# Shifted-window attention and a Fourier layer on one core: the first two images get an order of their own

## The chip, the cores and the metric

The kernel runs on one NeuronCore of a Trainium2 chip. The metric is the device time of one execution, in microseconds (us). All times of the profile are counted from the start of the program's span. TensorE, VectorE, ScalarE and GpSimd are called PE, DVE, ACT and POOL in the profile, and SP is the engine whose queue issues most DMAs.

## The reference

The input has 32 images of 56 x 56 positions with 128 channels in float32. Two layers follow each other, and both are residual: `x = x + f(group_norm(x))`.

```python
# layer 0: windows of 7 x 7 after a roll by 3, 4 heads of 32 channels
xs  = roll(gn(x), (-3, -3));  win = xs cut into 64 windows of 49 tokens
q, k, v = win @ w_qkv.T;      q *= 32 ** -0.5
a   = softmax(q @ k.T + bias(rpb_table) + shift_mask)
x   = x + roll(merge(a @ v) @ w_proj.T + b_proj, (3, 3))
# layer 1: along the width and along the height
y   = dct(gn(x))[..., :32];  y = einsum("bixy,ioy->boxy", y, w);  z = idct(y)
b   = relu((z_width + z_height) @ W1 + b1) @ W2 + b2
x   = x + b
```

The group norms take mean and variance over groups of four channels of a whole image, so an image's attention can start only when all of it has been read, and its second layer only when all of its attention is done.

## The kernel before, in words

The unit of work is a window row: 7 lines of an image, 8 windows, 392 tokens. An image has 8 rows, so there are 256 rows in all. The program is written as cycles. Cycle r does the scores of row r, the division and transposition of earlier rows, the values and the projection of row r - 3, and the sums for the second norm of row r - 4. From cycle 11 (`CONV_BEGIN`) on the second layer of an image runs beside the attention of later rows: its step c is cycle 11 + c for image 0 and 8 cycles later for each next image. Steps 0 to 2 transform (`transform`, `turn_modes`, `scale_modes`), steps 3 to 5 mix the modes (`mix`, result `z`), steps 5 to 7, 10 and 12 transform back (`modes_back`, `fetch_back`, result `xf`), and seven steps from 8 on are the feed-forward (`ff_in`, `ff_out`).

The order of PE, ACT, DVE and POOL is the order in which the program issues, cycle by cycle, written out by hand (`manual_schedule`). For SP that holds for the first 11 cycles only; later the planner places SP's DMAs. Each engine works through its own list in order and waits where an input or a buffer isn't ready.

What the change touches:

- The start. Image 0 is loaded in quarters, with 32 columns of channels at a time (`load_quarter`, L156, 16 loads on two queues). DVE turns these into channels by tokens (`turn_quarter`, L351 to L356) and takes statistics of each row (`row_stats`, L373). `image_norm` makes from them `ve` (L417), `rstd` on POOL (L421) and the scaled weights `wn` on ACT (L429), which the first product needs. POOL's queue also loads the position bias: seven loads into `rpb_cols` (L205), seven copies from there (L209) and one of the result into the other half (L212). DVE adds mask and bias in pieces (`bias_and_mask`, L230).
- A row. `attn_q` and `attn_k` (L450, L463 on ACT), `attn_scores` (products L498, addition of bias on DVE L506), `attn_max` (DVE L516, subtraction on POOL L517), `attn_exp` (ACT L523), `attn_recip` (DVE L528 and L530), `attn_divide` on POOL (L536 into the same buffer, or L547 into `blocks`), `attn_transpose`, `attn_values` (products L592), `attn_project` (products L637, addition of the residual on DVE L645, store to `scr`), `attn_sums` (DVE L662), `attn_squares` (POOL L677 or ACT L679), `sum_squares` (DVE L683), `attn_v` (products L476).
- `attn_transpose` has two ways. For rows below `TURNED_BY_PE` (16) PE multiplies by an identity (L563) and ACT copies the result out (L570). For later rows DVE transposes blocks (L575), and POOL's division writes them in six pieces.
- The PSUM banks of attention and of the second layer are two rings of four, taken in turn (`attn_bank`, `conv_bank`).
- SP loads the residual tokens of a row two cycles ahead (`load_tokens`), POOL adds the projection's bias to them (`add_bias`, L138), `back_weights` issues 12 small loads in each of two cycles and `ff_weights` six.

The order of a cycle on DVE in the first 11 cycles, which the change rewrites:

```python
attn_sums(last, j)                    # row - 4
attn_scores(im, i, cycle); attn_max(cycle)
attn_squares(last, j); sum_squares(last, j); add_sums(last, j)
divide(cycle)                         # softmax sums and division of row - 1
turn(cycle)                           # row - 2
attn_project(im3, i3)                 # residual of row - 3
```

## Time and profile before

| what | value |
|---|---|
| median of 3 runs | 3230.74 us (3228.96 to 3234.39) |
| the profiled execution's own time | 3231.41 us |
| its span | 3229.6 us |
| PE busy | 3145.1 us (97%) |
| DVE, POOL, ACT busy | 2517.3, 2297.7, 2184.8 us |
| PE busy in the first 240 us | 170.53 us |
| first product of attention | at 24.98 us |
| DMA queues | 448.47 MB, mean 139 GB/s |

The page gives the busy time of each engine over the whole span. A matmul of float32 appears as two records. An engine that is mostly busy over the span can still be idle in one stage, so busy times are read by stage here. The column PEclk is the clock that TensorE was granted, as a share of the full one.

### The profile page before, as it was taken

The page shows a single profiled execution, that of the slowest core. Times are in us where ns is not written, and L with a number is a line of the kernel's source. Part 1 is how long each engine was busy: PE and PEld are TensorE (multiplying, and loading weights), DVE is VectorE, ACT ScalarE, POOL GpSimd, SP SyncE. Part 2 cuts the span into 40 slices and gives each one's busy share as a digit, 9 for nine tenths or more (in the row PEclk, how much of TensorE's full clock was granted, in tenths as well). Part 3 has the DMA queues.
Part 4 walks back from the last instruction along what each step waited for, and adds up shares of the span by engine and source line. Part 5 has one row for each costly group of instructions (what it writes and reads, how often), then busy time and mean ns, then how long its engine had stood idle before and what let it go on. Part 6 is the DMA issues. An engine that isn't in the chain of part 4 may idle for free.

```text
span 3229.6 us, 152033 instructions
## 1 busy us (share of the span) xinstructions
PE 3145.1 (97%) x65664; PEld 2348.3 (73%) x65664; DVE 2517.3 (78%) x4764; ACT 2184.8 (68%) x4004; POOL 2297.7 (71%) x2570
## 2 busy tenths in 40 slices
PE   5789999999999999999999999999999999999999
PEld 4567777777777777777777777777777777777776
DVE  7678887888887888887888887888888888888751
ACT  4466777666777676776676777666776666777664
POOL 5467777777777777777777777777777777777741
PEclk9899999999999999999999999999999999999999
DMA  7446566656566655566656566556656656565443
GB/s 128 96 118 146 140 141 147 140 143 146 136 143 146 144 141 142 141 143 144 144 138 145 140 144 145 143 137 145 143 141 145 148 135 146 143 143 142 123 137 103
DMA packets 1171652, 448.47 MB, mean 139 GB/s; under 512 B 527690, under 2 KB 1141116, under 8 KB 1170980
## 3 DMA queue, kind: packets, MB, share of 16 engines
q1 hardware_dynamic: 1162788, 437.41, 56.9%
q8 instruction: 514, 8.42, 1.2%
q10 hardware_dynamic: 7584, 1.18, 0.3%
q14 instruction: 158, 1.29, 0.1%
q0 software_dynamic: 608, 0.17, 0.0%
HBM read 277.00 MB, written 161.48 MB: 136 GB/s over the span
## 4 chain that ended last, share of the span: by engine, by line
PE 95%; POOL 1%; DVE 1%; ACT 1%; issue 1%; DMA 1%; SPq 0%; DVEq 0%; ACTq 0%; POOLq 0%
PE pc L124 41%; PE pa L124 10%; PE pa L476 8%; PE pc L803 7%; PE pa L498 6%; PE pa L637 6%; PE pa L592 6%; PE pc L842 5%; PE pc L756 4%; PE pc L563 1%; PE pc L929 0%; ACT k L463 0%; PE pa L703 0%; POOL a L517 0%; DMA zT<-zscr 0%
## 5 line engine op out<-in xcount | busy, mean ns | idle before, releaser
L547 POOL TENSOR_TENSOR blocks<-a,rs 32x272 f32<-32x272 f32 (+3 forms) x1434 | 1219.6, 858 | 384.9 <-DVE rs L530 274.6
L124 PE MATMUL pc<-wff,hid 128*64 128x128 f32 x12288 | 713.1, 273 | 1.6 <-issue 0.6
L124 PE MATMUL pc<-xf,wff 128*64 128x512 f32 (+2 forms) x3584 | 714.5, 539 | 0.0
L124 PEld LDWEIGHTS pc<-wff,hid 128*64 128x64 f32 x12288 | 680.0, 137 | 8.4 <-issue 4.2
L517 POOL TENSOR_TENSOR a<-a,mx 128x784 f32<-128x784 f32 x250 | 376.6, 1507 | 294.8 <-DVE mx L516 269.3
L124 PEld LDWEIGHTS pc<-xf,wff 128*64 128x64 f32 x3584 | 263.7, 136 | 370.3 <-issue 295.7
L887 ACT ACTIVATE hid<-pc,b1sb 128x512 f32<-128x512 f32 (+2 forms) x896 | 500.6, 642 | 41.9 <-PE pc L124 41.6
L124 PE MATMUL pa<-xw,wn 128*64 128x392 f32 x2048 | 392.5, 498 | 29.1 <-ACT wn L429 28.5
L506 DVE TENSOR_TENSOR a<-pa,bm 128x392 f32<-128x392 f32 x500 | 259.0, 560 | 168.2 <-PE pa L498 155.5
L483 ACT COPY v<-pa 128x512 f32<-128x512 f32 x256 | 152.0, 594 | 283.7 <-PE pa L476 275.1
L463 ACT ACTIVATE k<-pa,bqkv,heads 128x392 f32<-128x392 f32 x512 | 318.9, 674 | 15.3 <-ACT q L450 1.1
L138 POOL TENSOR_TENSOR xr<-xr,bproj 128x384 f32<-128x384 f32 (+1 forms) x256 | 292.9, 1144 | 47.2 <-DMA xr<-in_x_dram 24.5
L892 POOL TENSOR_TENSOR res<-res,b2sb 128x512 f32<-128x512 f32 (+1 forms) x224 | 252.1, 1126 | 77.7 <-DMA res<-scr 57.1
L778 ACT ACTIVATE y<-modes,rstd 128x448 f32<-128x448 f32 x256 | 276.6, 1138 | 41.8 <-DVE modes L771 31.4
L450 ACT ACTIVATE q<-pa,bqkv 128x392 f32<-128x392 f32 x256 | 149.8, 585 | 229.0 <-PE pa L124 227.2
L523 ACT ACTIVATE a<-a 128x784 f32<-128x784 f32 x250 | 214.0, 856 | 130.3 <-POOL a L517 130.0
L575 DVE STREAM_TRANSPOSE eT<-blocks 128x1024 f32<-128x1024 f32 x240 | 295.1, 1230 | 0.0
L592 PEld LDWEIGHTS pa<-eT,v 49*32 49x32 f32 x16384 | 173.0, 106 | 157.9 <-issue 70.8
L528 DVE TENSOR_REDUCE sm<-a 128x16 f32<-128x784 f32 x250 | 239.8, 959 | 56.0 <-ACT a L523 55.9
L476 PE MATMUL pa<-wn,xw 128*64 128x128 f32 x4096 | 281.8, 279 | 1.6 <-issue 1.2
L516 DVE TENSOR_REDUCE mx<-a 128x16 f32<-128x784 f32 x250 | 242.2, 969 | 7.7
L476 PEld LDWEIGHTS pa<-wn,xw 128*64 128x64 f32 x4096 | 219.8, 137 | 36.6 <-issue 2.3
(126 smaller groups left out, 4978.6 us busy)
## 6 DMA issues: line engine op xcount, KB each, us to landing
zscr<-z SPq DMA_DIRECT2D x512, 112.0 KB
xin<-in_x_dram SPq DMA_DIRECT2D x480, 112.0 KB
htok<-scr SPq DMA_DIRECT2D x128, 392.0 KB
zT<-zscr SPq DMA_DIRECT2D x192, 256.0 KB
res<-scr SPq DMA_DIRECT2D x160, 256.0 KB
out_dram<-res SPq DMA_DIRECT2D x160, 256.0 KB
scr<-x SPq DMA_DIRECT2D x256, 112.0 KB
xr<-in_x_dram SPq DMA_DIRECT2D x256, 84.0 KB
```

The costliest lines, as they stand in the source:

```text
L124: nc.tensor.matmul(dst[ps], lhsT=lhsT[:, ps], rhs=rhs, start=start, stop=stop)
L138: nc.gpsimd.tensor_tensor(piece, piece, bproj.unsqueeze(1).to_broadcast([P, n, C]), ALU.add)
L463: nc.scalar.activation(k_sb[:, u], pk[:, :RT].rearrange("p (w j) -> p w j", j=WT), AF.Identity, bias=im.bias[:, 3 + u : 4 + u], scale=head ...
L476: nc.tensor.matmul(pv[HALVES[w % 2], w // 2 * C : (w // 2 + 1) * C], lhsT=im.half[i // NP][:, t0 : t0 + JP], rhs=im.w[:, 2 * C : 3 * C], s ...
L506: nc.vector.tensor_tensor(a[:, 2 * hp : 2 * hp + 2, :, 0:WT].rearrange("p u w j -> p w u j"), ps[hp][:, :RT].rearrange("p (w u j) -> p w u ...
L517: nc.gpsimd.tensor_tensor(a3, a3, mx.unsqueeze(2).to_broadcast([P, 2 * NWR, WT]), ALU.subtract)
L547: nc.gpsimd.tensor_tensor(dst[to, k, :, :n], a3[src, :, kb * KB : kb * KB + n], rs[src].unsqueeze(2).to_broadcast([src.stop - src.start, 2 ...
L575: nc.vector.transpose(eT.rearrange("p t (k j) -> p k t j", k=2), blocks[r % 2])
L592: nc.tensor.matmul(po4[u][h * HD : (h + 1) * HD, pr], lhsT=v[ks, pr, h * HD : (h + 1) * HD], rhs=eT[ks, h * NP + pr, :WT], start=True, sto ...
L778: nc.scalar.mul(y[:, r], t.rearrange("p (n k) -> p n k", k=NM), im.rstd)
L887: nc.scalar.activation(hf[:, :n], ph[:, :n], AF.Relu, bias=b1sb[:, f : f + 1])
L892: nc.gpsimd.tensor_tensor(im.res[:, :k], im.res[:, :k], b2sb.unsqueeze(1).to_broadcast([P, k, C]), ALU.add,)
```

## The change

- **Start.** Image 0 is loaded by lines of tokens (`load_lines`, ten loads on the queues of SP and ACT) into the buffers `y_of`, and PE turns it: `turn_lines` multiplies each line by `turned_in`, an identity whose columns are rolled by three. ACT copies the result into the row layout, and DVE takes the statistics from PSUM.
- **Queues.** The copies into `rpb` move from POOL's queue to SP's (`place_rpb`), ahead of the loads of image 1. The loads of the second layer's transform matrices and of `gavg` move behind those of the mixing weights, and `bproj` moves from ACT's queue to SP's.
- **Rows 0 to 10** (`first_rows`). The division takes row r - 2 in place of r - 1 and stands early in the cycle. The squares of row r - 4 stand ahead of the subtraction, and the residual addition stands ahead of the softmax sums of the next division. Quarters and statistics of the next image move, and the norm's steps are taken earlier.
- **Rows 11 to 18** (`next_rows`). These cycles get an order of their own in place of the general one. The sums and scalings of the second layer are placed in it one by one, and the planner still places SP's DMAs.
- **Row 19.** The last cycle before the general order puts the squares of its finished row late and takes image 1's second statistics behind the feed-forward.
- **Transposition.** `TURNED_BY_PE` becomes 19, so rows 16 to 18 are transposed by PE too. The identity lies in `blocks[0]`, which POOL clears in cycle 20.
- Image 2's quarters are turned in cycles 8 and 9 with its statistics in 10, in place of cycles 8 and 9.

```diff
-TURNED_BY_PE = 2 * NWR
+TURNED_BY_PE = 2 * NWR + 3
...
-    for k in range(2):
-        for u in range(2):
-            xins[0, k, u] = load_quarter(0, k, u)
+    for n0, n1 in ((0, 2 * NQ), (2 * NQ, 3 * NQ), (3 * NQ, NCH)):
+        load_lines(n0, n1)
...
+    def turn_lines(im, p):
+
+        k = p // 2
+        slots = im.half[k][:, : NWR * WS * ROWS[k]]
+        slots = slots.rearrange("p (j h s) -> p h j s", j=NWR, s=WS)
+        banks = [(conv_bank, attn_bank)[k]() for _ in range(2)]
+        for n in range(NQ):
+            for r, ps in enumerate(LINE):
+                nc.tensor.matmul(
+                    banks[r][:, n * S : (n + 1) * S],
+                    lhsT=lines_of(p)[ps, n],
+                    rhs=turned_in[ps],
+                    start=True,
+                    stop=True,
+                )
+        for r, t in enumerate(banks):
+            h = 2 * NQ * p + r + (SS if k == 0 else WS - S // 2)
+            nc.scalar.copy(
+                slots[:, h : h + 2 * NQ - 1 : 2],
+                t[:, :RT].rearrange("p (n j s) -> p n j s", n=NQ, s=WS),
+            )
+            nc.vector.bn_stats(im.st[:, 2 * p + r], t[:, :RT])
...
     def first_rows(cycle):
...
+        divide_row(cycle - 2)
         if last:
-            attn_sums(last, j)
-        if cycle >= NWR:
-            next_quarter(cycle)
+            attn_squares(last, j)
...
+        attn_scores(im, i, cycle)
+        attn_max(cycle)
...
         if last:
-            attn_squares(last, j)
+            attn_sums(last, j)
             sum_squares(last, j)
             add_sums(last, j)
-        divide(cycle)
...
         turn(cycle)
         if im3:
             attn_project(im3, i3)
...
+    def next_rows(cycle):
+        c = cycle - CONV_BEGIN
...
+        attn_exp(cycle - 1)
+        scale_head(first, c, False)
+        next_quarter(cycle)
+        attn_values(im3, i3, cycle - 3, i in VALUES_BY_ACT)
+        tokens_bias(cycle)
+        if c == 0:
+            for h in range(2):
+                transform(first, True, h)
...
+        attn_scores(im, i, cycle)
+        attn_max(cycle)
+        for h in range(2 if c == 0 else 0):
+            for r in range(2):
+                turn_modes(first, True, h, r)
+        for r in range(2):
+            columns_turn(cycle, r)
+        turn(cycle)
+        for width, g in back_groups(c):
+            modes_back(first, width, g)
+            fetch_back(first, width, g)
+        if c == 3:
+            half_columns(cycle)
+        if c:
+            attn_squares(last, j)
+            attn_sums(last, j)
+        divide(cycle)
...
+        attn_v(im, i, cycle)
...
+        half_columns(cycle, True)
+        scale_head(first, c, True)
+        load_back(cycle + 1)
+        next_begin(cycle)
+        attn_project(im3, i3)
...
+    for cycle in range(CONV_BEGIN, HEAD_END):
+        next_rows(cycle)
+    for cycle in range(HEAD_END, NB * NWR + CONV_BEGIN + FF_AT[-1] - NWR + 1):
+        halves_first(cycle)
```

## The prediction

> **What bounds the kernel now.** I read the page first.
>
> ```profile
> span 3229.6 us, 152033 instructions
> PE 3145.1 (97%) x65664; PEld 2348.3 (73%) x65664; DVE 2517.3 (78%) x4764; ACT 2184.8 (68%) x4004; POOL 2297.7 (71%) x2570
> PE   5789999999999999999999999999999999999999
> PEclk9899999999999999999999999999999999999999
> ```
>
> TensorE is idle for 3229.6 - 3145.1 = 84.5 us, and the first slices hold most of it. So I asked for busy time by stage. Columns: stretch, its length, then PE, PEld, DVE, ACT, POOL busy, granted clock, DMA share, GB/s.
>
> ```profile
> 36.00:72.00 36.00, 28.13 (x768) 21.88 (x768) 26.32 (x46) 23.82 (x47) 18.80 (x16) 1.00 0.42 129
> 93.00:113.00 20.00, 13.71 (x344) 11.93 (x346) 12.55 (x21) 6.70 (x16) 7.79 (x7) 0.67 0.46 83
> 113.00:134.00 21.00, 15.11 (x366) 10.58 (x362) 12.88 (x24) 9.84 (x22) 13.13 (x12) 0.83 0.44 96
> 202.00:240.00 38.00, 34.58 (x836) 23.93 (x838) 29.88 (x61) 25.07 (x45) 31.25 (x36) 1.00 0.49 114
> 240.00:330.00 90.00, 89.33 (x1882) 68.12 (x1880) 72.97 (x136) 61.01 (x114) 66.79 (x75) 1.00 0.61 145
> ```
>
> The reader is to see that TensorE is full from 240 us on, and that no engine is full before. TensorE is busy 170.53 of the first 240 us, so 69.5 us are idle there: 25 ahead of its first product, 44.5 after. The clocks of all stages between 25 and 202 us add up to 41.4 us at half rate. Only these 240 us can be won.
>
> Then the timeline of the start, and the waits between 30 and 240 us (in total, times, longest).
>
> ```profile
> 14.61 3.88 POOL L209 DMA_DIRECT2D rpb<-rpb_cols  x7 [2.21 <-DMA rpb_cols<-in_rpb_rev_dram]
> 20.82 0.58 POOL L212 DMA_DIRECT2D rpb<-rpb  x1 [1.92 <-DMA rpb<-rpb_cols]
> 21.05 0.15 DVE L417 SCALAR_TENSOR_TENSOR ve<-back 128x1 f32<-128x1 f32 x1
> 23.68 0.60 POOL L421 TENSOR_TENSOR rstd<-ve,mhalf 128x1 f32<-128x1 f32 x1
> 24.98 1.57 PE L124 MATMUL pa<-xw,wn 128*64 128x392 f32 x4 [24.98 <-ACT wn L429]
> ```
> ```profile
> DVE part L683 <- POOL sq L677: 20.8, 10, 2.7
> PE pa L592 <- DVE x L645: 16.6, 6, 4.7
> DVE xw L351 <- DMA xin<-in_x_dram: 4.6, 2, 3.9
> ```
> ```profile
> 113.05 1.50 POOL L517 TENSOR_TENSOR a<-a,mx 128x784 f32<-128x784 f32 x1 [2.98 <-DVE mx L516]
> 114.51 1.04 POOL L677 TENSOR_TENSOR sq<-x 128x512 f32<-128x512 f32 x1
> 115.58 0.69 DVE L683 TENSOR_REDUCE part<-sq 128x32 f32<-128x512 f32 x1 [2.70 <-POOL sq L677]
> 116.18 0.96 DVE L528 TENSOR_REDUCE sm<-a_extra 128x16 f32<-128x784 f32 x1
> 117.35 0.56 DVE L645 TENSOR_TENSOR x<-pa,xr 128x384 f32<-128x384 f32 x1
> ```
>
> The start: `rstd` was ready to compute at 21.2 but waited 2.5 us behind the bias copies in POOL's queue. The rows: VectorE waits for the squares, which stand behind POOL's subtraction; behind that wait stands the residual addition L645, and behind it the PSUM bank that the next row's values need. I count rows by their row maxima L516: rows 0, 2, 10, 11, 18, 21 begin theirs at 31.86, 43.14, 121.22, 136.41, 217.02, 253.34. Rows 3 to 10 take 9.8 us each, the loop add 1.04, max 0.97, wait 2.6, sums 0.6, softmax sums 1.2, residual 0.65, values 0.8, scores 0.9 = 8.8, and what transposes of the next image (2.15) fall in it.
>
> **The start, part by part.** Image 0 came as 12,544 pieces of 128 B in 16 loads; now 3,136 of 512 B in ten. A packet of the middle of the run (600 to 700 us: 58.7% of 16 x 100 us by 37,077 packets, 377 B on average) takes 25 ns, so 3,136 x 25 / 16 = 5 us. Before, the last quarter reached VectorE at 14.90. The last rows are small loads which wait for loads eight earlier; I put their landing at 9 us (8 to 12). TensorE then turns the last seven lines. There are 56 turns, two records each. The nearest row is L563 (64 records of 49 columns, half as wide: 2.07 us), so all 112 take 4.1 us, 8.3 at half clock, of which the last quarter (2.1) lies on the path. ScalarE's two copies (L570, 0.5) add 1.1, the last statistics 0.5, the chain to `ve` 2.5 (18.72 to 21.20), `rstd` 0.6, weights 0.7: first product at 16.5, not 24.98. POOL no longer holds `rstd`: the eight bias copies go to SP, ahead of image 1's loads. They wait there for `rpb_cols`; landed at 14.6 before, about 11 now that the queues empty earlier. Then 7 x 0.42 issue, 2.3 landing, the copy of the copies 2.1: 18.4. Of 24 bias sums (L230, 4.74 us) 20 follow: 22.4. Row 0's scores are added then, not at 30.79: 8.4 us earlier (bounds 4 and 10).
>
> **Rows 0 to 10.** Rows 1 to 3 stay bound by VectorE (bias sums 2.86, transposes): maximum of row 3 at 42.2, before 50.15. From row 4, squares go ahead of the subtraction, the quotient is of two rows back, and the residual goes ahead of softmax sums. Two loops remain. TensorE: q and k 1.4, values 0.9, wait for ScalarE's k 0.35, scores 0.9, transposes 2.0, projection 0.8, v 0.9 = 7.25. VectorE: 1.04 + 0.97 + 0.6 + 0.6 + 0.6 + 1.2 = 5.0, plus 2.15 in the rows with a quarter = 7.2. I take 7.4. ScalarE (0.6 + 1.25 + 0.86 + 1.43 + 1.0 + 0.6 = 5.7) and POOL (1.5 + 1.5 + 1.2 + 1.0 + 0.3 = 5.5) stay under it. SP's 24 weight loads (53.72 to 61.86, 73.11 to 80.75) and six more (4.3) block stores and tokens as before, now in shorter rows: from row 2's store 59.5 SP reaches image 2's first quarter at 76.2, it is usable 5.3 later (94.17 to 99.51 before), and row 8 waits: 14 us, not 7.4. `nb`, on which TensorE waited 5.47 us there, is ready. Row 10 at 101, before 121.2: 20 us earlier. Moving gavg and dct behind w0 costs nothing: row 11 is the first to use them.
>
> **Rows 11 to 18.** Row 11: TensorE's transposes need a bank that VectorE frees only after two modes transposes: 9.3 of work + 3.3. Rows 12 to 18, each by its fullest engine: 9.5, 10.5, 12 (ScalarE: scale, shift, wrap, four z), 9.5, 11.8 (ScalarE: xf, z), 10.3, 11.5 (VectorE: statistics, xf) = 75.1; before 80.6. Row 18 at 188.6: 28.4 earlier.
>
> **Rows 16 to 18 by TensorE.** 3 x 2.07 = 6.2 us more of TensorE; VectorE loses 3 x 1.23, POOL 3 x 1.7. Bounds 0 and 6.2; two of the three fall where TensorE is full: 4.1. Clearing `blocks` (0.93 of POOL) and the later sums of row 19 lie under TensorE's work; uncovered, 1 to 2 us.
>
> **After row 21** every engine's instructions stand in the same order as before, so nothing per image changes.
>
> **The clock.** A gap of 2.71 us ahead of 72.39 was followed by half rate (L498 1.56 instead of 0.89 us); one of 2.02 at 61.2 was not. The Trainium skill, "TensorE: Matmul & The Clock Gate", section "HAM oscillation — how this bites in real kernels", sets the limit at idle gaps of about 3.4 us. By it only row 8's wait would be slow: some 5 us at half rate, 2 lost. By the row, row 11 and the gaps of rows 0 to 3 count too: 12 us, 4 lost. I take the row.
>
> **The sum**, by TensorE to row 21: before, 253.3 - 69.5 = 183.8 busy; 41.4 at half rate, about 0.71 busy, cost 14.7: 169.1 at full rate. After: start 16.5 + 169.1 + 6.2 + idle (rows 0 to 3 8.7, rows 4 to 10 8, row 11 3.3, rows 12 to 18 10.5, later 1 = 31.5) + clock 4 = 227.3: 26 us less. The rows' sum gives 28.4 - 4.1 = 24.3. I take 26.5: the profiled execution's own 3231.4 becomes 3204.9. The median of the runs, 3230.7, is 0.7 lower: 3204.
>
> **The rivals.** (1) Orders tighter than I think: rows 11 to 18 near TensorE's own 73 us, row 8 covered. Idle 17, clock 2: 211, 42 us less, 3189. For it: no engine's sum reaches its row. Against: in-order banks. Chance 0.14. (2) SP and ScalarE take the place: loads late in rows 5 to 8, each row 11 to 18 two engines in series, 12 us as before. Only start and rows 3 to 7 stay: 8 + 6 - 4 = 10 less, 3221. For it: SP's 8 us blocks, POOL's in-order token additions. Chance 0.10. (3) Slower: ScalarE in rows 11 to 18 becomes one chain with TensorE. Mixing waits for the scaling in front of it, and q for z behind it. Price: ScalarE's 10 to 11 us plus TensorE's 6.9 less what overlaps. It decides when these eight rows average 12 + (16 + 6.5) / 8 = 14.8 us against 12 now; at 15.5, 12 us slower, 3243. Against: rows 12 to 15 took 10 to 13 with the same work. Chance 0.03. (4) The turn isn't earlier, since small loads land late, and rows don't shorten: 3229. Chance 0.03.
>
> **How the numbers follow.** The forecast has 0.70. Its bounds (start 4 to 10, rows 0 to 10 by 5 us, rows 11 to 18 by 6, transposes 0 to 6) give 3192 to 3216; I reach to 3189 and 3219, leaving out about 1 in 10 on each side. A measurement here tells 0.2% (6.5 us) from no change. Faster takes forecast, (1), (2): 0.93 with a little left out.
>
> **What would show it.** First product by 18 us; L677's wait gone; rows 4 to 7 at 7.4 us; half clock under 15 us; row 18 before 195; from row 21 the same pace, 97 us an image. Wrong: row 18's maximum after 205, rows 4 to 7 above 9, or a different pace later.

## The result, and the profile after

| what | before | after |
|---|---|---|
| median, the changed kernel's own runs | 3230.47 us | 3222.48 us (3219.83 to 3228.9, 13 runs) |
| ratio, with its 95% interval | | 0.9976 [0.9967, 0.9984] |
| the same once more, in later runs (e12) | 3232.31 us | 3226.3 us, 0.9982 [0.9973, 0.9990] |
| the profiled execution's own time, span | 3231.41, 3229.6 us | 3222.57, 3220.8 us |
| first product of attention | 24.98 us | 23.31 us |

The change brings 6 to 8 us where 26.5 were forecast; 3219 was the upper end of what the prediction gave. These are lines of the page of the kernel after:

```profile
span 3220.8 us, 152669 instructions
...
PE 3162.6 (98%) x65968; PEld 2369.0 (74%) x65968; DVE 2508.5 (78%) x4753; ACT 2189.3 (68%) x4018; POOL 2280.0 (71%) x2552
```

TensorE is idle for 3220.8 - 3162.6 = 58.2 us instead of 84.5. So 26 us of idle time did go, about what the forecast's sum had. But TensorE is busy 17.5 us longer, and that is the sum to explain. Busy time by stage, the kernel after (columns: stretch, its length, then PE, PEld, DVE, ACT, POOL busy, granted clock, DMA share, GB/s):

```profile
5.40:18.30 12.90, 12.80 (x112) 12.49 (x112) 3.48 (x8) 3.70 (x9) 7.62 (x20) 1.00 0.46 90
...
82.00:102.00 20.00, 15.97 (x404) 13.50 (x404) 11.19 (x20) 10.29 (x25) 9.99 (x11) 0.84 0.63 130
...
227.00:317.00 90.00, 89.47 (x1906) 68.69 (x1904) 71.62 (x132) 61.00 (x116) 66.11 (x76) 1.00 0.60 141
```

The three rows are the turn, rows 8 and 9, and the 90 us from row 20's maximum on. The first is new: TensorE is full from 5.40 to 18.30 us with the 112 records of the turn, and its weight loads (PEld) are full too. In the second TensorE is idle for 4 us of 20, and the clock of 0.84 puts some 6 us at half rate (before, rows 8 and 9 had 0.67). The last reads like its counterpart of before: TensorE is full. Next, the start, from the timeline of the kernel after:

```profile
5.40 6.62 PE L400 MATMUL pc<-turned_in,y 56*128 56x56 f32 x55 [5.40 <-DMA y<-in_x_dram]
...
11.82 6.38 PE L400 MATMUL pa<-turned_in,y 56*128 56x56 f32 x55
...
20.18 10.99 SPq L160 DMA_DIRECT2D y<-in_x_dram  x16
...
21.81 0.15 DVE L486 SCALAR_TENSOR_TENSOR ve<-back 128x1 f32<-128x1 f32 x1
...
22.04 0.57 POOL L490 TENSOR_TENSOR rstd<-ve,mhalf 128x1 f32<-128x1 f32 x1 [6.23 <-DVE ve L486]
...
23.31 1.58 PE L129 MATMUL pa<-xw,wn 128*64 128x392 f32 x4 [5.11 <-ACT wn L498]
```

GpSimd no longer holds `rstd`: it waits 6.23 us for `ve`. But `ve` comes at 21.81, later than the 21.05 of before, because the turn ends at 18.2. The first product takes 1.58 us for four records, which is half rate. Image 1's loads start at 20.18 behind the bias copies (seven from 12.05 on, and the copy of the copies into the other half at 19.35). The waits between 30 and 240 us (in total, times, longest):

```profile
PE pa L661 <- DVE x L714: 10.1, 7, 3.4
...
DVE part L752 <- POOL sq L746: 3.2, 3, 2.1
```

The wait of VectorE for the squares fell from 20.8 to 3.2 us, and TensorE's for the residual from 16.6 to 10.1. Both were forecast. Other waits in rows 7 to 9 took their place (TensorE's timeline: start and length; in brackets how long it waited, and for what):

```profile
79.50 3.66 PE L632 MATMUL pc<-blocks,a_extra 128*64 128x49 f32 x64 [2.18 <-POOL a_extra L605]
...
100.00 3.65 PE L632 MATMUL pc<-blocks,a 128*64 128x49 f32 x64 [1.09 <-POOL a L605]
```

In row 7 TensorE waits for the quotient, because seven small instructions of the norm stand ahead of the softmax sum on VectorE. The transposes that follow take 3.66 us instead of 2.07: half rate. In row 8 VectorE waits 2.99 us, until 91.87, for image 2's quarter.

### The profile page after: what moved, and what is told of

Same layout as the page of the kernel before. It is cut to its first block, busy times and chain, and to the rows that moved or that the text cites. A ratio compares the mean times of both kernels' runs of the same rounds, so it can differ in the third digit from the quotient of the medians.

```text
span 3220.8 us, 152669 instructions
## 1 busy us (share of the span) xinstructions
PE 3162.6 (98%) x65968; PEld 2369.0 (74%) x65968; DVE 2508.5 (78%) x4753; ACT 2189.3 (68%) x4018; POOL 2280.0 (71%) x2552
## 4 chain that ended last, share of the span: by engine, by line
PE 94%; DVE 2%; issue 1%; DMA 1%; POOL 1%; ACT 1%; SPq 0%; DVEq 0%; POOLq 0%; ACTq 0%
PE pc L129 41%; PE pa L129 10%; PE pa L545 8%; PE pc L872 7%; PE pa L567 6%; PE pa L706 6%; PE pa L661 5%; PE pc L911 5%; PE pc L825 3%; PE pc L632 1%; DMA xin<-in_x_dram 1%; PE pc L998 0%; ACT k L532 0%; PE pa L772 0%; PE pc L400 0%
## 5 line engine op out<-in xcount | busy, mean ns | idle before, releaser
L616 POOL TENSOR_TENSOR blocks<-a,rs 32x272 f32<-32x272 f32 (+3 forms) x1416 | 1202.3, 856 | 379.1 <-DVE rs L599 257.1
L961 POOL TENSOR_TENSOR res<-res,b2sb 128x512 f32<-128x512 f32 (+1 forms) x224 | 251.8, 1124 | 83.4 <-DMA res<-scr 77.8
L847 ACT ACTIVATE y<-modes,rstd 128x448 f32<-128x448 f32 x256 | 276.8, 1141 | 44.8 <-DVE modes L840 31.3
L597 DVE TENSOR_REDUCE sm<-a 128x16 f32<-128x784 f32 x249 | 238.5, 958 | 45.9 <-ACT a L592 45.3
```

What stands on the lines that cost most here:

```text
L616: nc.gpsimd.tensor_tensor(dst[to, k, :, :n], a3[src, :, kb * KB : kb * KB + n], rs[src].unsqueeze(2).to_broadcast([src.stop - src.start, 2 ...
L847: nc.scalar.mul(y[:, r], t.rearrange("p (n k) -> p n k", k=NM), im.rstd)
L961: nc.gpsimd.tensor_tensor(im.res[:, :k], im.res[:, :k], b2sb.unsqueeze(1).to_broadcast([P, k, C]), ALU.add,)
```

## The stages, kernel by kernel

The table cuts each profiled execution at the maxima of rows 0, 10 and 21 and of the last row (255), in us. It holds the experiments too, which follow.

| kernel | row 0 at | rows 0 to 10 | rows 10 to 21 | row 21 to the last | ratio |
|---|---|---|---|---|---|
| before | 31.9 | 89.4 | 132.1 | 2833.5 | 1 |
| after | 30.9 | 80.2 | 130.5 | 2835.4 | 0.9976 |
| after, again (e12) | 30.4 | 83.4 | 133.3 | 2838.5 | 0.9982 |
| turn in halves (e1) | 27.2 | 79.7 | 136.0 | 2831.0 | 0.9970 |
| old start (e2) | 33.8 | 79.0 | 131.9 | 2833.6 | 0.9988 |
| old rows 0 to 10 (e3) | 31.0 | 95.9 | 134.2 | 2835.2 | 1.0033 |
| the same, image 2 as before (e14) | 30.9 | 89.1 | 133.7 | 2831.4 | 1.0019 |
| old rows 11 to 19 (e4) | 31.0 | 77.8 | 138.1 | 2835.3 | 0.9987 |
| rows 16 to 18 by DVE (e5) | 30.7 | 80.7 | 134.0 | 2830.2 | 0.9981 |
| products ahead of the turn (e6) | 31.3 | 79.9 | 136.3 | 2830.9 | 0.9970 |
| halves, bias on POOL's queue (e7) | 26.8 | 78.0 | 135.4 | 2828.8 | 0.9964 |
| and norm behind the sums (e8) | 27.1 | 80.1 | 134.9 | 2826.9 | 0.9962 |
| that again (e16) | 26.9 | 78.6 | 133.9 | 2825.9 | 0.9965 |
| that, last lines first (e11) | 28.6 | 79.1 | 137.6 | 2833.4 | 0.9972 |
| that, products behind the turn (e15) | 27.5 | 79.9 | 135.4 | 2830.2 | 0.9972 |
| new rows 0 to 10 alone (e9) | 34.1 | 80.1 | 134.4 | 2838.8 | 0.9988 |
| new start alone (e10) | 31.1 | 89.4 | 135.1 | 2831.2 | 1.0006 |
| new rows 11 to 19 alone (e13) | 33.7 | 89.9 | 144.6 | 2831.0 | 1.0036 |

The two profiles of the changed kernel differ by 5.6 us at row 21 and by 8.7 us at the last row. So one profile tells a stage's length to a few us, and the time is read from the ratios. The profiled execution isn't always one of middling time: in e1, e2, e14 and e16 it is the fastest of the kernel's runs, in e6, e9, e12 and e13 the slowest (e13's took 3246.08 us, with a median of 3237.4). The ratios tell two kernels apart only so far: the intervals of e2 and e4 touch both of those that the changed kernel has.

## The experiments

**The turn in halves (e1).** The theory here is that the turn sets the start, and not the landing of the loads. Each line's product is cut into two of 64 channels, the form of the row that the prediction had scaled.

```diff
-                    banks[r][:, n * S : (n + 1) * S],
-                    lhsT=lines_of(p)[ps, n],
+                    banks[r][hs, n * S : (n + 1) * S],
+                    lhsT=lines_of(p)[ps, n, hs],
```

> The changed kernel with each line turned in two halves of 64 channels instead of one product with 128 columns of weights. Weight theory: the turn takes 13.0 us because a record's weight load of 128 columns takes 330 ns and 56 lines have 112 of them; halves load into separate columns beside each other, the turn falls to 6 to 8 us, and the first product stands at 17 to 19 us instead of 23.3. Row 0's scores are then held by the bias sums (their input lands near 22.5), so row 0's maximum moves from 30.9 to 28 to 29 and the total falls by 2 to 3 us. Clock theory: the turn is slow because TensorE works at half rate until 34 us; halves leave it at 13 us or make it longer, the total within 1 us.

3222.45 us, 0.9970 [0.9959, 0.9982], not to be told from the changed kernel. The turn fell from 12.8 to 7.7 us (5.36 to 13.10), with twice as many records. A stretch of it in the columns of the busy times above, then two lines of the timeline:

```profile
6.70:11.70 5.00, 5.00 (x194) 5.00 (x190) 2.89 (x7) 2.98 (x6) 2.36 (x4) 1.00 0.79 152
```
```profile
5.36 3.70 PE L401 MATMUL pc<-turned_in,y 56*64 56x56 f32 x109 [5.36 <-DMA y<-in_x_dram]
...
18.53 1.58 PE L129 MATMUL pa<-xw,wn 128*64 128x392 f32 x4 [5.43 <-ACT wn L499]
```

In the trace's single records, two of the changed kernel's (one of each of two lines) start within 7 ns of each other, and the next two 213 ns later. In e1 four (two lines, two halves) start within 20 ns, and the next four 107 ns later. So four narrow records run beside each other where two wide ones do, and the turn's own pace is twice as fast; the rest of its 7.7 us is mostly waiting for lines.

The first product comes 4.8 us earlier, row 0's maximum 3.7. So the turn did set the start. At row 21 the lead over the changed kernel is gone (242.9 against 241.6), which lies within what two profiles of one kernel differ by.

**The old start (e2).** Loading by quarters and queues as before, everything else new.

```diff
-    for n0, n1 in ((0, 2 * NQ), (2 * NQ, 3 * NQ), (3 * NQ, NCH)):
-        load_lines(n0, n1)
+    for k in range(2):
+        for u in range(2):
+            xins[0, k, u] = load_quarter(0, k, u)
```

> The changed kernel with the start of the kernel before: quarters of 128-byte pieces, turned by VectorE, bias copies on POOL's queue, transform matrices early. Theory of the lost start: by the rows' maxima the new start is only 0.9 us ahead, so without it the total stays within 1.5 us of the changed kernel's. The prediction's view, that the start is worth 8 us: the total rises to about 3230.

3228.11 us, 0.9988 [0.9982, 0.9995]. Row 0 comes 2.9 us later than in the changed kernel and row 21 3.2 later. Leaving the new start out costs 2 to 4 us here, not 8.4. But this isn't quite the start of before. In the changed kernel the order written by hand holds from the first line of the program on (L86), in the kernel before only from the turning of image 0 on, and e2, e9 and e13 keep the new place. In their lists GpSimd's loads of the masks and its clears stand behind the bias copies, so `rstd` comes at 24.8 to 25.2 us (23.68 before) and row 0 about 2 us later than in the kernel before. So up to 2 us of the times of these three runs can be this list's.

**The old rows 0 to 10 (e3), and image 2 placed as before (e14).** In e3 `first_rows` has the old order. Image 2's steps stay where the change puts them: one quarter in cycle 8, one in 9. In e14 they go back too:

```diff
-        if b == 1:
-            steps[0] = ((0, 0), None, ())
-            steps[1] = ((0, 1), None, ())
-            steps[2] = (None, None, (0, 1, 2, 3))
```

> The changed kernel with rows 0 to 10 in the order of the kernel before. Order theory: the early squares, quotients and residual are worth the 9 us by which row 10's maximum came ahead; without them rows 3 to 10 take 9.5 us each again, and the total rises to 3230 to 3232. Rival: the time comes back in rows 11 to 18, which wait less then; the total rises by 3 us or less.

> The changed kernel with the old order of rows 0 to 10 as in the earlier run that was 10 us slower than before, but with image 2's two quarters and its statistics in cycles 8 and 9 as before, not in 8, 9 and 10. Theory 1, placing them later is what made rows 8 and 9 take 15 us each there (VectorE waited 15.3 us for quarters, SP reached them late): row 9 at 112 instead of 117, time at or below before (0 to 4 us less). Theory 2, the order of rows 11 to 18 behind old rows 0 to 10 does it: row 9 earlier or not, time still 8 us or more above before.

e3 took 3242.03 us, 1.0033 [1.0021, 1.0045]: slower than before. e14 took 3233.61 us, 1.0019 [1.0012, 1.0025]. Rows 0 to 10 take 95.9 us in e3, 89.1 in e14, 89.4 before. The old order and the new placing clash, and the cause is in the queue of SP. First e3, then e14 (SP's and VectorE's timelines):

```profile
107.37 0.78 SPq L722 DMA_DIRECT2D scr<-x  x2
...
108.31 3.55 SPq L160 DMA_DIRECT2D xin<-in_x_dram  x4
...
114.19 1.09 DVE L424 STREAM_TRANSPOSE xw<-xin 128x512 f32<-128x512 f32 x1 [6.12 <-DMA xin<-in_x_dram]
```
```profile
99.92 2.09 SPq L160 DMA_DIRECT2D xin<-in_x_dram  x4
```

In e3 the second quarter's loads stand behind a row's store at 107.37, which waits for its residual, and VectorE then waits 6.12 us for them. In e14 they leave at 99.92, ahead of that store (106.61). So the placing explains 7 us of rows 0 to 10, and by the ratios some 4.5 us of the time. It does not explain why e14 is still slower than before.

**The old order of rows 11 to 19 (e4).** The general order from cycle 11 on, as before, with PE transposing rows 16 to 18.

```diff
-    for cycle in range(CONV_BEGIN, HEAD_END):
-        next_rows(cycle)
-    for cycle in range(HEAD_END, NB * NWR + CONV_BEGIN + FF_AT[-1] - NWR + 1):
+    for cycle in range(CONV_BEGIN, NB * NWR + CONV_BEGIN + FF_AT[-1] - NWR + 1):
```

> The changed kernel with rows 11 to 18 in the general order of the later rows, as before. Order theory: the own order is worth the 8 to 9 us that its rows' maxima gained between row 10 and row 18, so the total rises to about 3231. Rival: the maxima stand earlier within their cycle in the own order, and 3 to 5 of these us are given back between rows 18 and 21; its worth is 3 to 5 us, total 3226 to 3227.

3227.98 us, 0.9987 [0.9980, 0.9994]. Rows 10 to 18 take 97.4 us against 86.7. A good part of that is no time: in the own order a row's maximum stands earlier among TensorE's work, and rows 18 to 21 then take 40.7 us against 43.7. From row 10 to row 21 it is 138.1 against 130.5 (133.3 in the second profile of the changed kernel, e12), and by the ratios 2 to 4 us.

**Rows 16 to 18 transposed by VectorE (e5).**

```diff
-TURNED_BY_PE = 2 * NWR + 3
+TURNED_BY_PE = 2 * NWR
```

> The changed kernel with rows 16 to 18 transposed by VectorE again (TURNED_BY_PE back at 16). Price theory: three rows cost TensorE 2.07 us each, and the lead of the rows' maxima falls by 7.4 us between rows 18 and 21, where TensorE is full; without them the total falls by 4 to 6 us, to about 3219 where the changed kernel has 3224. Rival: rows 16 to 18 aren't bound by TensorE, and VectorE's 1.23 us and POOL's division in pieces (3.2 instead of 1.5 us) make these rows longer by what TensorE saves; the total stays within 2 us.

3221.07 us, 0.9981 [0.9974, 0.9987]: not to be told from the changed kernel. TensorE's 6.2 us of transposes are gone, and yet nothing is won. GpSimd now divides these rows in six pieces of together 5.34 us, and rows 18 to 21 show what that holds (GpSimd and TensorE of e5, then the wait of VectorE between them: total, times, longest):

```profile
211.73 5.34 POOL L616 TENSOR_TENSOR blocks<-a,rs 128x512 f32<-128x512 f32 x6
...
220.65 1.08 PE L129 MATMUL pc<-xf,wff 128*64 128x512 f32 x4 [2.13 <-DVE res L1008]
```
```profile
DVE res L1008 <- POOL res L961: 6.3, 1, 6.3
```

The division stands ahead of the subtraction (217.15) and of `res` (218.61), VectorE waits 6.3 us for that, and TensorE waits for VectorE. Behind these waits TensorE stood at half rate (granted clock 0.53 from 222 to 233 us). Row 20's maximum comes 20.8 us after row 19's, against 15.2 in the changed kernel, where the division at this place is one instruction of 1.51 us (at 207.54).

So in the own order TensorE's transposes pay for themselves: they cost 6.2 us of TensorE and take about as much of waiting and half rate away.

**Products ahead of the turn (e6).** Three products of zeros with 512 columns, before the turn, so that TensorE is busy from 3.65 us on.

```diff
+    warm_up(3)
     images[0] = image_begin(0)
```

> The changed kernel with three more products of 512 columns on zeros ahead of the turn of image 0, which keep TensorE busy from about 4 to 8 us (their results are overwritten). Clock theory: TensorE is then at full rate when the lines arrive, and the second half of the turn takes 3.5 us instead of 6.4. Weight theory: the weight loads of 128 columns set the pace at either clock, the second half stays at 6 to 6.5 us. The total isn't expected to move by more than 3 us either way.

3218.01 us, 0.9970 [0.9958, 0.9981]. The turn in two halves of 56 records:

```profile
3.65 5.48 PE L169 MATMUL pa<-warm 128*128 128x512 f32 x6 [3.65 <-DVE warm L165]
...
9.07 3.33 PE L408 MATMUL pc<-turned_in,y 56*128 56x56 f32 x56
...
12.24 6.02 PE L408 MATMUL pa<-turned_in,y 56*128 56x56 f32 x56
```
```profile
12.30:18.20 5.90, 5.90 (x58) 5.78 (x56) 2.60 (x7) 1.95 (x4) 3.35 (x13) 0.51 0.08 15
```

The first half runs at 59 ns a record, the second at 108, as in the changed kernel (116), though TensorE was never idle between them. The clock granted to the second half was 0.51 of the full one. So the turn's price is the half rate and the wide form together. And the turn's own products, in this wide form, did not hold the full rate. The 5.5 us of products ahead of it took the gain away: the first product comes at 23.73.

**Halves, and the bias copies on POOL's queue (e7).** The seven copies into `rpb` go back to POOL's queue, behind the masks' loads, which move behind GpSimd's clears, so that image 1's first loads leave SP at once.

```diff
-                nc.sync.dma_start(
+                nc.gpsimd.dma_start(
                     rpb[iy * WS : (iy + 1) * WS], cols[:, :, WS - 1 - iy : span - iy]
                 )
-            nc.sync.dma_start(rpb[JP : JP + WT], rpb[0:WT])
...
+        if k:
+            nc.sync.dma_start(rpb[JP : JP + WT], rpb[0:WT])
```

> The turn in halves of 64 channels, and the position bias taken off SP: POOL issues the seven copies behind its memsets, SP only the last one, behind the first half of image 1's loads. Queue theory: in the turn in halves alone, image 1's loads start at 20.5 us because SP waits for the bias from 12 to 20 us, so tokens, mixing weights and with them rows 1 to 8 stay where they were; now they start near 11, end near 23, row 3's maximum moves from 47.8 to 44 or 45, and the total falls by 2 to 4 us against the halves alone. Rival: rows 1 to 3 are bound by VectorE's own work, and the early loads change nothing; total within 1.5 us of the halves alone.

3217.03 us, 0.9964 [0.9951, 0.9976]. Image 1's first loads start at 9.71 instead of 20.18, row 3's maximum comes at 45.3 (49.6 in the changed kernel) and row 10's at 104.8 (111.1). The last 14 records of the turn waited until 11.89 us for the last small loads. From 9.57 us on four records take 59 ns instead of 107: this turn reached the full rate. With e1 and e6 that gives the time from one group of records on two lines to the next (two records in the wide form, four in halves; the turn has 56 such groups):

| products with | at half rate | at full rate |
|---|---|---|
| 128 channels | 213 ns (changed kernel) | 112 ns (first half of e6) |
| halves of 64 | 107 ns (e1) | 59 ns (e7, 9.57 to 10.39 us) |

Width and clock each make a factor of about 2. And now the bias copies hold row 0 (VectorE's timeline of e7):

```profile
21.49 3.96 DVE L268 TENSOR_TENSOR bm<-rpb,mask 49x98 f32<-49x98 f32 x20 [1.63 <-DMA rpb<-rpb]
```

**And the norm step behind the sums (e8, again e16).** The seven small instructions that stood ahead of row 7's softmax sum move behind it.

```diff
         divide_row(cycle - 2)
+        if cycle == NWR - 1:
+            norm_step(cycle)
...
         attn_v(im, i, cycle)
-        if cycle == NWR - 2:
-            norm_step(NWR - 1)
```

> As the run before, and in cycle 7 the second step of image 1's norm (seven small instructions of VectorE) stands behind the softmax sums of row 5 instead of ahead of them. Theory: these seven delay POOL's quotient, TensorE waits 2.18 us at 79.5 for it and then goes to half rate for 6.8 us; moved, the wait falls under 1 us, no half rate follows in row 7, and the total falls by 2 to 4 us. Rival: row 8 waits for image 2's first quarter anyway, so what row 7 wins is waited there; the total stays.

> The fastest version once more, on the chip of the run with products between. If 0.9962 holds, 12 us below before, row 21's maximum at 240 to 243; if the earlier ratio was luck of scatter, 0.9970 to 0.9978 as the other kernels with the new rows.

3215.18 us, 0.9962 [0.9948, 0.9975], and in later runs 3215.82 us, 0.9965 [0.9951, 0.9978]. It is not to be told from e7. TensorE's wait in row 7 did fall, from 2.18 to 0.74 us, but row 8 then waited longer: from row 6's maximum to row 8's it takes 22.5 us in e7, 21.7 in e8, 22.7 in e16. The rival was right. The two runs agree, and with e7 they are the fastest found: about 11.5 us below before, where the changed kernel has 6 to 8. The intervals of the two kernels still touch.

**The new rows 0 to 10 alone (e9) and the new start alone (e10).** Each is the kernel before with one part of the change, and with the order by hand from the first line on: e9 has the edits of e2, e4 and e5 together, e10 those of e4, e5 and e14. The identity lies in a buffer of its own again, as before.

```diff
-    ident = blocks[0].rearrange("p k t c -> p (k t c)")[:, :P]
+    ident = work.tile([P, HB], F32, tag="hid", name="ident", bufs=NF)[:, :P]
```

> The kernel before with the new order of rows 0 to 10 alone: start, rows 11 to 18, row 19 and the transposes of rows 16 to 18 are the old ones. The knock-outs so far cost 4 (start), 18 (rows 0 to 10), 3.6 (rows 11 to 18) and 0 to 2 us (transposes), 26 in all against a gain of 8. Theory 1, the parts need each other and the knock-outs of the other three add: row 21's maximum at 241.6 + 3.2 + 5.3 + 3.9 = 254, time as before within 2 us. Theory 2, the order of rows 0 to 10 brings its gain by itself: row 10 at 112.8 as with the old start, then 96 us to row 18 as before, so row 18 at 209 and row 21 at 245, time 6 to 8 us below before. Theory 3, it brings by itself what leaving it out cost: 18 us below before.

> The kernel before with the new start alone (image 0 turned by TensorE, the bias copies on SP's queue); all rows in the old order. Theory 1, the start's gain is small and adds: row 0's maximum at 31 (before 31.9), row 10 within 2 us of 121, time 0 to 4 us below before. Theory 2, what made the kernel without the new rows 0 to 10 slower by 9 us is the new start, which lets image 1's loads come 1.6 us later than before and so holds rows 2 to 10: row 10 at 124 or later, time 5 us or more above before.

e9: 3228.18 us, 0.9988 [0.9979, 0.9996], 4 us below before, though its row 0 comes 2.2 us later (see e2). e10: 3234.31 us, 1.0006 [0.9998, 1.0015], no gain. In the stages the parts do add: the new rows 0 to 10 take 80.1 us alone and 80.2 within the change (before 89.4), and the new start alone gives a row 0 at 31.1 and leaves rows 0 to 10 at 89.4. So neither is held back by the other.

**The new rows 11 to 19 alone (e13).** The edits of e2, e5 and e14 together, so `next_rows` and row 19 as in the changed kernel, and all else as before but for the order by hand from the first line on. The loop that e4 took out is what stays:

```diff
+    for cycle in range(CONV_BEGIN, HEAD_END):
+        next_rows(cycle)
```

> The kernel before with the new order of rows 11 to 18 and of row 19 alone: start, rows 0 to 10 and the transposes of rows 16 to 18 are the old ones. Theory 1, this order by itself brings what leaving it out cost: row 11 to row 18 in 79 us instead of 80.6, row 10 unchanged at 121, time 4 us below before. Theory 2, this order does harm behind the old rows 0 to 10 (the kernel without the new rows 0 to 10 was 10 us slower than before, the new start alone about equal): time 5 to 10 us above before, row 18 at 222 or later.

3237.4 us, 1.0036 [1.0023, 1.0049]: 10 to 12 us slower than before; its row 0 already comes 1.8 us later (see e2). Rows 10 to 21 take 144.6 us instead of 132.1 in the profile, which is that of the slowest run. Two things stand in it. With VectorE transposing, row 20 again comes 20.8 us after row 19 (233.4 to 254.2), as in e5. And rows 11 and 12 run at half rate: the granted clock is 0.76 from 123 to 152 us, against 0.97 from 119 to 144 in e14. Both have a wait of 2.9 us for the modes; ahead of it TensorE waited 2.59 us for the residual in e13 and 1.40 in e14. So the third part alone does harm. Whether the transposes by TensorE would take it away was not run: e14 has them behind the old rows 0 to 10 and is slower than before too, and e5 loses nothing without them behind the new rows.

**The last lines' loads first (e11), and products behind the turn (e15),** both on top of e8.

```diff
-    for n0, n1 in ((0, 2 * NQ), (2 * NQ, 3 * NQ), (3 * NQ, NCH)):
+    for n0, n1 in ((3 * NQ, NCH), (0, 2 * NQ), (2 * NQ, 3 * NQ)):
```
```diff
             turn_lines(images[0], p)
         half_windows(images[0], k)
+    warm_up(4)
```

> The fastest kernel so far (turn in halves, bias copies on POOL's queue, norm step behind the sums: 0.9962 of before) with the six small loads of the last lines issued ahead of the four large ones. There the last 14 records of the turn waited for them until 11.9 us. Theory 1, the small loads were late because they wait for loads ahead of them: the turn ends by 11.5 us instead of 13.6, the first product starts at 17 instead of 19, and the time falls by up to 2 us. Theory 2, the bias copies decide row 0 now (landed 21.5, then 4 us of additions, scores at 25.7): the first product is earlier, row 0's maximum stays at 26.7 and the time within 1 us. Theory 3, the large loads are late in turn and the turn begins 2 us later: no gain at all.

> The fastest version (turn in halves, bias copies on POOL's queue, norm step behind the sums) with four products of zeros, 512 columns each, between the turn and the first product, where TensorE stood idle for 5.4 us. They add work and change no result. Theory 1, the half rate of the first products costs time: the first product takes 0.8 us instead of 1.57, row 3's maximum comes 2 to 3 us earlier (45.3 there, here 43), and the time falls by 2 to 4 us. Theory 2, VectorE's additions of bias and mask set rows 0 to 3: row 0's maximum moves by less than 0.7 us, row 3's by less than 1, the time by nothing that shows.

e11: 3223.3 us, 0.9972 [0.9961, 0.9982]. The turn no longer waits within itself, but it starts at 9.31 us instead of 5.2, since the large loads land later, and the first product comes at 20.96. The third theory was right. e15: 3219.32 us, 0.9972 [0.9961, 0.9983]. The first product runs at full rate, and that buys nothing (TensorE's timeline, e15 first, then e16 without the products):

```profile
13.82 6.24 PE L169 MATMUL pc<-warm 128*128 128x512 f32 x8
...
19.99 0.88 PE L129 MATMUL pa<-xw,wn 128*64 128x392 f32 x4
...
23.45 0.89 PE L579 MATMUL pa<-k,q 64*49 64x98 f32 x32 [1.62 <-ACT k L544]
```
```profile
18.50 1.58 PE L129 MATMUL pa<-xw,wn 128*64 128x392 f32 x4 [5.48 <-ACT wn L502]
...
23.46 1.56 PE L571 MATMUL pa<-k,q 64*49 64x98 f32 x32 [1.53 <-ACT k L536]
```

The products ended 1.5 us after `wn` was there, so row 0's scores start at the same 23.45. Row 0's maximum is at 27.5 against 26.9, row 3's at 48.1 against 45.4 in e16 and 47.5 in e8; e15 and e8 fell back to half rate at 35 to 36 us and e16 did not. VectorE's additions of bias and mask end only at about 25.5 us in e7's trace, so for row 0 a TensorE at half rate is hidden behind them here.

**The changed kernel again (e12).**

> The changed kernel itself, on the chip of these runs, to set the kernel with the early lines beside it: 0.9976 of before as in its own runs (interval 0.9967 to 0.9984), row 21's maximum at 241.6 within 1 us.

3226.3 us, 0.9982 [0.9973, 0.9990]. Row 21's maximum lay at 247.1, 5.6 us later than in the first profile. TensorE stood at half rate for about 31 us between 30 us and there, instead of 17, and was idle for 44.1 us instead of 42.6.

## Why the prediction was wrong, point by point

By TensorE up to row 21's maximum the books close. Before: 183.9 us busy and 69.5 idle. After: 199.0 busy and 42.6 idle, in all 11.8 us less. Busy time grew by 15.1: the turn 12.8, the transposes 6.2, the first rows at half rate about 3.7 (an estimate), less some 8.5 for half rate later (12 stretches of 3.4 us became 5, at 0.71 busy and half the speed), which makes 14.2.

The prediction's sum by rows had row 21's maximum 24.3 us earlier, and it came 11.8 earlier. The 12.5 us between are, by the rows' maxima: 7.4 lost by row 3 (the start), 2.7 in rows 4 to 10, 0.9 won in rows 11 to 18, and 3.3 lost in rows 19 to 21. From row 21 to the end of the profiled execution 3 us more went (8.8 left), with nothing in the order of the engines to explain it. The 26.5 us that the prediction took lay above both of its own sums, 26 and 24.3.

- **The start is the step that failed**, above all in one term: the turn. The prediction scaled 64 records of 49 columns at full rate (2.07 us) to 4.1 us for 112, at most 8.3, with 2.1 on the path. It measured 12.8, and all of it lay on the path: TensorE began at 5.40 and was never out of work. The scaled row has products of 64 channels; the turn's have 128, which doubles the time, and the half rate nearly doubles it again (table of e7). That TensorE starts at half rate stood in a line that the prediction shows: the first product took 1.57 us for four records, against 0.88 in e15. What follows the turn was forecast well: 5.1 us to the first product, against 5.4. It came at 23.31, not 16.5, and row 3's maximum at 49.6, not 42.2. The loads' landing, put at 9 us, had no share in this: the turn outlasted them. In e7, with a shorter turn, the last ones were waited for until 11.89, at the edge of the range of 8 to 12.
- **A better turn brings part of that back,** as far as the rows go. With halves and early loads (e7, e8, e16) row 0 comes 4 us earlier than in the changed kernel, row 3 2 to 4 and row 10 4 to 6. By the ratios the time falls by some 4 to 6 us, though the intervals touch. That the turn wins these us isn't shown: at row 21 the three profiles are between 2.2 us ahead of the changed kernel and 0.5 behind, and the rest of their lead arises after row 21, where every engine's order is the same.
- **The bias copies** are the next term that was too small. The prediction put them at 18.4 landed and saw no price in SP's queue. In the changed kernel VectorE's additions began at 23.02, right behind the norm, so the landing itself cost 0.2 us at most. But with the shorter turn the additions wait for the last copy, until 21.98 in e1 and 21.49 in e7. So even a turn as short as forecast would not have brought row 0 to the forecast place. The copies also held image 1's loads until 20.18 (18.57 before). From e1 to e7 they leave SP, and these loads start 10.7 us earlier; row 10 comes 2.2 us earlier, and the ratios differ by 2 us, within their intervals. In the kernel before, `rstd` waited last for clears in GpSimd's list (`q`, `a` and `blocks`, 21.40 to 23.72), which stood behind the copies.
- **Rows 0 to 10** took 80.2 us in place of 89.4: 9 us, and e9 has the same alone. Forecast were 20 less 8.4 for the start, so 11.6. Most of the squares' wait went, as written, and rows 4 to 7 took 7.3 us on average (7.4 forecast). Rows 4 to 10 together are 2.7 us longer than forecast. Row 8 took 15.9 us (14 forecast), for the quarter, as forecast. Row 10 took 11.0 (7.4 forecast), and half rate from 99 to 106 us lies in it. The norm's small instructions in row 7, which the prediction didn't cost, are not it: moved away, they leave row 8 where it was (e8).
- **Rows 11 to 18** took 86.7 us (87.6 forecast). That is luck too: row 11 took 8.2 us (12.6 forecast), and rows 12 to 18, priced by the fullest engine of each, 78.5 (75.1). And part of this lead is position: the maximum stands earlier among TensorE's work than before, and the lead comes back in rows 19 to 21.
- **Rows 18 to 21** took 43.7 us instead of 36.3, 7.4 more. The prediction had 4.1, for two of three transposes. Most of all three fell where TensorE is full: 254 records more than before lie in this stretch, 158 of them transposes. But e5 shows that without them the time is the same, and its trace has GpSimd's division in pieces and half rate in their place. The bound "0 to 6.2" held, though for a reason that the prediction didn't name.
- **The clock.** 17 us at half rate after 30 us of the first profile (12 forecast), about 31 in the second. The row ruled and not the limit of 3.4 us that the prediction set beside it: half rate followed a wait of 2.18 us at 79.50. The length of a wait alone doesn't decide it, though: 2.85 us in e14 (at 132.11) left the full rate, and e8 lost it at about 76 us behind waits of 0.3 and 0.74. Not reckoned for the first rows was that TensorE starts at half rate: products ran so until about 34.5 us. In e15's kernel that price was hidden; in the changed kernel VectorE waited 1.89 us for row 0's scores, which is what it can have cost there.
- **The idle time after the first product** was 32 us (31.5 forecast), and that is luck: rows 0 to 3 had 5.5 us (8.7 forecast), rows 4 to 10 9.3 (8), row 11 1.2 (3.3), rows 12 to 18 15.5 (10.5), later 0.6 (1).
- **After row 21** "nothing changes" is not refuted: the stretch to the last row lasted between 2826 and 2839 us over all kernels, two profiles of the changed kernel differ by 3.1 there, and TensorE's idle time in it was 4 to 14 us, most of it put to "issue". e7, e8 and e16 have the shortest stretches (2826 to 2829, idle 4 to 7). What TensorE waits for there is shown below this list.
- **The rivals.** The second rival's time, 3221, is where the result lies. Its mechanism was not the one: SP and ScalarE did not take the place in rows 11 to 18. The third rival, own rows that make things slower, is what e13 shows of that part alone, by what it didn't name (GpSimd's pieces ahead of `res`, and half rate).

**The waits after row 21.** The traces point to what TensorE waits for there: its next block of instructions. The page of the kernel after has 517 transfers of kind "instruction" on queue q8 (count, MB, share), 16 KB each, which is one for every 256 of TensorE's 132,409 instructions. Below it stands one such wait (TensorE's timeline):

```profile
q8 instruction: 517, 8.47, 1.2%
```
```profile
1078.48 0.44 PE L911 MATMUL pc<-idctw,zT 64*64 64x112 f32 x9 [1.24 <-issue]
```

In the 18 traces 313 waits of over 0.1 us between row 21 and the last row are put to "issue". Counted through TensorE's instructions, every one of them comes 193 or 194 behind a multiple of 256, and a transfer of q8 began about 2.1 us ahead of it (1.0 to 3.1). They sum to 9.7 us in the changed kernel, 13.0 in e12 and 3.2 to 6.4 in e7, e8 and e16, and over the 18 traces the length of the stretch goes with that sum (correlation 0.96). What makes the sum larger or smaller stays open, and with it a few us of every total.

What else stays open: e14 is 6 us slower than before by its runs. Its profile, even with before at row 21, is of the fastest of its 21 runs (3230.04 us, median 3233.61), so it doesn't show where. And the parts alone (e9 -4, e10 +2, e13 +10 to +12 us) do not sum to the whole (-6 to -8). Up to 2 us each of e9 and e13 can be GpSimd's list at the start. The new rows 11 to 19 win at most 2 to 4 us behind the new rows 0 to 10 (e4) and nothing behind the old ones (e14, e13); no run shows why.

## What to carry to other kernels

When a product has no like in the trace, take the nearest row of the same width and form, and price it at the clock that TensorE will have at that place: here, at the start, that was half rate, and the first product's own duration said so. A stage that begins when its data lands and never waits lies on the path in full. A lead read at one marker instruction is a lead in time only where the same work lies ahead of it in both kernels, so count records as well as microseconds. Taking work off the fullest engine wins nothing where what replaces it holds an engine that it waits for (e5). A lead that arises where nothing was changed isn't the change's, so read where in the trace it arises before you give it a cause. And when parts of a change are taken out, compare what is left with the kernel before, instruction by instruction (e2).

## What the runs showed of the hardware

- Products of 56 rows by 56 columns with 128 channels kept TensorE busy for 12.8 of 12.9 us and stayed at half rate: 116 ns a record, against 59 after three wide products. After 3.3 us of such products the full rate was lost again (108 ns, granted clock 0.51), with no idle time between (e6). In halves of 64 channels, with twice the records, the turn had the full rate from 9.57 us on in e7: 15 ns a record, and 27 until then.
- Products of half the width on two lines started together: four records within 20 ns in e1. Those of full width started two by two, and such a turn took twice as long.
- The clock column read 1.00 in the first 30 us, while products took half rate's 1.58 us for four records (0.88 in e15). A clock that the records have not yet seen change is not a measured one; the duration of a known product is.
- Half rate came after waits far shorter than its own stretches of 3.4 us: after 2.18 us at 79.50, and after waits of 1.55 and 1.09 us in a row at 97 to 100 us. A longer one, of 2.85 us in e14, was not followed by it.
- Where TensorE was full, nearly all of its idle time came at one place in every 256 of its instructions, about 2 us after a transfer of the instruction queue began: 9.7 of 10.9 us from row 21 to the last row in the changed kernel.
